# An implicit-filter convolution with a scored normalization: two orders changed in a software-pipelined loop over channels

## The chip, the cores and the metric

The kernel runs on one core of a Trainium2 chip. The metric is the device time of one launch in microseconds (us), as a median over runs. "Slot" below means four 64x64 matmuls that use the four quarters of the TensorE array at the same time.

## What is computed

For each of C = 64 channels, four images of 256 x 256 (float32) go through two layers. Layer 0 makes, from two small sine networks, one filter per axis, hx and hy; their outer product is a 2D filter, applied as a causal 2D convolution, and a bias times the input is added. Layer 1 forms scores of the rows, weighs and sums them, adds the sums to the rows, and normalizes each channel over all images.

```python
k = einsum('ijk,imk->ijmk', hx, hy)[0]                  # hx, hy: decayed sine networks
y = irfft2(rfft2(x, 512) * rfft2(k, 512) / 512)[:256, :256]   # causal 2D convolution
x = y + x * bias[:, None, None]
scores = einsum('bpsd,bptd->bpst', x, x) / sqrt(256)
red = sum(scores * weights[None], axis=-1, keepdims=True)
y = x + red
mean, var = mean(y, (0, 2, 3)), var(y, (0, 2, 3))       # per channel
out = (y - mean) * rsqrt(var + 1e-5) * gamma + beta
```

The filter being separable, the 2D convolution is two 1D convolutions, each a matrix product with a Toeplitz matrix.

## The kernel before

**Data.** A channel's four images lie as [128 partitions, 2 pairs v, 4 column groups, 256], two images in the two halves of the partitions. The filters are computed once, written to DRAM (g_dram), and each channel's Toeplitz tile (toep, `hs[c]`, four buffers) is read from there by four DMAs of 52 KB (`load_h`, L203) into partitions 0 to 63; `copy_h` (L208) copies them to partitions 64 to 127 on ScalarE (ACT). The input comes in four DMAs of 256 KB per channel (`load_xt`, L76), the weights in one of 320 KB (`load_w`, L82, on ACT's DMA queue), and the result leaves in four DMAs of 256 KB (`finish`, L616 and its DMA L617).

**The order is written by hand.** The scheduler is off; every engine runs its instructions in the order in which the program lists them. A loop over c = 0 to 61 works, in each pass ("period"), on several channels at once: the first convolution z of channel c+1, the second convolution x0 of channel c, G (the scores) of channel c, and the sums, the normalization and the output of channels c-1 to c-4 (in the code p, q, f, e).

**TensorE (PE) in one period**, 52 slots:
1. x0, first half (`conv_x0`, `x0_slots`, L323): 8 slots of 256, 192, 128, 64, 256, 192, 128, 64 columns into the PSUM tile p2_0.
2. x0's second half (p2_1) alternating with z's first half (`z_slots`, L263, p1_0, 8 slots of 256, 128, 64, 64 columns twice over): 16 slots.
3. z's second half (p1_1): 8 slots.
4. G's first half (`gram`, L392): four slots of 192 columns, four of 128.
5. G's second half: the same 8 slots, with four slots of 64 columns of the *shared product* for channel c+2 among them (`shared_slots`, L234). `take` draws from both in turn until the shorter is used up.

The shared product is a part of z that two block rows have in common: the sum of two column groups (`sums`, L225, on VectorE) times one Toeplitz block. `keep_shared` (L243) copies it from PSUM to SBUF on ACT, and `add_shared` (L278, VectorE) adds it to z in the next period.

**PSUM** is one pool of four slots of two banks each, shared by p2_0, p2_1, p1_0, p1_1, the two G tiles and the shared product. Each slot is handed on when its last reader is done.

**VectorE (DVE) in one period:** `add_bias` (L344) of x0's two halves, `add_red` (L499) twice, L278 twice, small steps of the normalization, and `weigh_pair` on each G tile (four L429 and one L418), with `turn_rows` (a transpose, L463) in the second.

**ACT:** an output at five places in the period, `parts_of(c, 0)` to `parts_of(c, 4)` (place 4 is empty but for the last channels), `pick_red` (L492), `root` (three small steps), `copy_h`, the copies of z (L272), the mean and the squares (L547 to L552), and, at the end, `keep_shared`.

**GpSimd (POOL):** `sum_squares` (L558), the accumulating DMA `add_rows` (L473), `sum_means` (L505) and the long reduction `all_sum` (L483), which `pick_red` of the next period reads.

**The rows' way.** `keep_rows` writes the transposed row sums to DRAM from SyncE's (SP's) queue (L468); `add_rows` on POOL adds them into pr from there; `all_sum` then reduces pr. SP issues, in this order: rows, first output, xt, two Toeplitz loads, output, xt, two Toeplitz loads, output, xt, output, xt. An output's DMA waits there for ACT, the rows' for DVE, with all later ones behind it.

Of the kernel before, what the change touches and what calls it, by code (L numbers as in the profile page):

```python
# [15 lines left out]
B, C, S = 4, 64, 256  # L16
# [25 lines left out]
def conv_scores_bn_kernel(  # L42
# [29 lines left out]
    def load_xt(c, v, n):  # L72
        if c not in xts:
            xts[c] = ld.tile([P, 2, 4, S], F32, tag="xt", name=f"xt_{c}", bufs=4)
        part = bass.ts(n, 2)
        nc.sync.dma_start(xts[c][:, v, part], xT[c, v, :, part])  # L76
# [117 lines left out]
    def load_h(c, n):  # L194


        if not n:
            hs[c] = ld.tile([P, ROW], F32, tag="toep", name=f"toep_{c}", bufs=4)
        src = bass.AP(
            g_dram.tensor, g_dram.offset + c * GL + 16 * n,  # L200
            [[4 + C * GL, COPIES], [1, 4], [1, ROW]],
        )
        nc.sync.dma_start(hs[c][bass.ts(n, 16)], src)  # L203
# [12 lines left out]
    def pair_of_banks(name):  # L216
        return ps.tile([P, 2, 2, S], F32, tag="ps", name=name)
# [9 lines left out]
    def shared_slots(c, both):  # L227

        toep = hs[c].rearrange("p (b s) -> p b s", s=H)
        for k in range(4):  # L230
            for t in range(4):
                u, v = t % 2, t // 2
                rows = bass.ts(u, H)
                nc.tensor.matmul(  # L234
                    both[bass.ts(v, H), u, k], lhsT=xss[c][rows, v, bass.ts(k, H)],
                    rhs=toep[rows, 11], start=(k == 0), stop=(k == 3),
                )
            yield

    def keep_shared(c, both):  # L240

        kept[c] = wk.tile([P, 2, 2, P], F32, tag="kept", name=f"kept_{c}")
        nc.scalar.copy(  # L243
            kept[c].rearrange("p m u s -> p u m s"),
            both[:, :, :4].rearrange("p u (m k) s -> p u m (k s)", k=2),
        )
# [57 lines left out]
    def take(*slots):  # L304

        slots = list(slots)
        while slots:
            slots = [s for s in slots if next(s, s) is None]

    def copy_z_plain(c, m, p1):  # L310
        for u in range(2):
            nc.scalar.copy(zs[c][:, m, u], p1[:, u, :, ::-1])

    def x0_slots(c, z, m, p2):


        toep = hs[c]
        for i in range(2):
            for k in range(4):
                for t in range(4):  # L320
                    v, u = t % 2, t // 2
                    rows = bass.ts(v, H)
                    nc.tensor.matmul(  # L323
                        p2[bass.ts(u, H), v, i, : S - H * k],
                        lhsT=z[rows, k // 2, u, k % 2, bass.ts(2 * m + i, H)],
                        rhs=toep[rows, H * k : S], start=(k == 0), stop=(k == 3),
                    )
                yield

    def conv_x0(c, z, m):  # L330
        p2 = pair_of_banks(f"p2_{c}_{m}")
        take(x0_slots(c, z, m, p2))
        return p2
# [35 lines left out]
    def begin(c):  # L369
        x0 = wk.tile([P, 2, 4, S], F32, tag="x0", name=f"x0_{c}", bufs=5)  # L370
        red0 = reds[c % 3][:, : 2 * B].rearrange("p (b n) -> p b n", n=2)
        sp = wk.tile([P, B, S], F32, tag="sp", name=f"sp_{c}")
        pr = wk.tile([P, B, S], F32, tag="pr", name=f"pr_{c}")
        rd = wk.tile([P, B, S], F32, tag="rd", name=f"rd_{c}")
        st8[c] = (x0, red0, sp, pr, rd)
# [3 lines left out]
    def gram_slots(c, v, gs):  # L379


        xb = st8[c][0].rearrange("p v i (t s) -> p v i t s", s=H)
        for places in (
            ((0, slice(0, 3), slice(0, 5, 2)), (1, slice(1, 4), slice(2, 7, 2))),
            ((2, slice(2, 4), slice(3, 7, 3)), (3, slice(0, 4, 3), slice(0, 4, 3))),
        ):
            for i in range(4):
                for n in range(4):
                    u, h = n % 2, n // 2
                    rows = bass.ts(u, H)  # L390
                    m, t, o = places[h]
                    nc.tensor.matmul(  # L392
                        gs[bass.ts(h, H), u, o, :],
                        lhsT=xb[rows, v, i, m, :], rhs=xb[rows, v, i, t, :],
                        start=(i == 0), stop=(i == 3),
                    )
                yield
# [67 lines left out]
    def keep_rows(c):  # L465

        rows[c] = dram.tile([P, 32], F32, name=f"rows_{c}")
        nc.sync.dma_start(rows[c], acrosses.pop(c))  # L468

    def add_rows(c):  # L470

        pr = st8[c][3]
        nc.gpsimd.dma_start(  # L473
            pr[0:1].rearrange("p b (n q i) -> p (b n) q i", n=2, i=32),
            rows.pop(c).rearrange("(q j) i -> j q i", q=4)[None, : 2 * B], accum_op=ALU.add,
        )
# [11 lines left out]
    def pick_red(c, v=None):  # L488

        rd = st8[c][4].rearrange("p (v u) s -> p v u s", u=2)  # L490
        pairs = slice(0, 2) if v is None else v
        nc.scalar.copy(rd[H:, pairs, 0, :], rd[H:, pairs, 1, :])  # L492
# [63 lines left out]
    def sum_squares(c, mom):  # L556
        tot = sm.tile([P, 3], F32, tag="tot", name=f"tot_{c}")
        nc.gpsimd.partition_all_reduce(tot[:, 0:2], mom[:, 6:8], P, RED.add)  # L558
        return tot
# [248 lines left out]
    def begin_z(c):  # L808
        zs[c] = wk.tile([P, 2, 2, 2, S], F32, tag="z", name=f"z_{c}")
# [21 lines left out]
    for c in range(C - 2):  # L831
        p, q, f = c - 1, c - 2, c - 3
        short = c + 1 > 1
        begin(c)
        begin_z(c + 1)
        z = zs.pop(c)
        if p >= 0:
            keep_rows(p)
        if f >= 0:
            tot = sum_squares(f, moms[f])  # L840
        if p >= 0:
            add_rows(p)
        parts_of(c, 0)
        if c + 3 < C:
            load_xt(c + 3, 0, 0)
            for n in range(2):
                load_h(c + 3, n)
        if c:
            p2 = conv_x0(c, z, 0)
            add_bias(c, 0, p2)  # L850
        else:
            first_x0(z)
        if q >= 0:
            pick_red(q)
        if f >= 0:
            scales[f] = root(f, tot)
            steps = scale_steps(f, moms.pop(f), *scales.pop(f))
        else:
            steps = iter(())
        parts_of(c, 1)  # L860
        if c + 3 < C:
            load_xt(c + 3, 1, 0)
            for n in range(2, 4):
                load_h(c + 3, n)
        copy_h(c + 2)
        if c + 2 < C - 1:
            sums(c + 2)
        if q >= 0:
            add_red(q, 0)
        next(steps, None)  # L870
        slots = []
        if c:
            p2 = pair_of_banks(f"p2_{c}_1")
            slots.append(x0_slots(c, z, 1, p2))
        p1 = [pair_of_banks(f"p1_{c + 1}_0")]
        slots.append((z_slots if short else plain_slots)(c + 1, 0, p1[0]))
        take(*slots)
        copy_any = copy_z if short else copy_z_plain
        copy_any(c + 1, 0, p1[0])
        if c:  # L880
            add_bias(c, 1, p2)
        next(steps, None)
        parts_of(c, 2)
        if c + 3 < C:
            load_xt(c + 3, 0, 1)
        if q >= 0:
            add_red(q, 1)
            sum_means(moms[q])
        if p >= 0:
            all_sum(p)  # L890
        next(steps, None)
        p1.append(pair_of_banks(f"p1_{c + 1}_1"))
        take((z_slots if short else plain_slots)(c + 1, 1, p1[1]))
        copy_any(c + 1, 1, p1[1])
        load_w(c + 1, nc.scalar)
        for m in range(2):
            if short:
                add_shared(c + 1, m, p1[m])
            next(steps, None)
        for _ in steps:  # L900
            pass
        if q >= 0:
            minus_mean(moms[q])
            squares(q, moms[q], 0)
        parts_of(c, 3)
        if c + 3 < C:
            load_xt(c + 3, 1, 1)
        if q >= 0:
            squares(q, moms[q], 1)
        parts_of(c, 4)  # L910
        gram(c, 0)
        slots = []
        if c + 2 < C - 1:
            both = ps.tile([P, 2, 8, H], F32, tag="ps", name=f"shared_{c + 2}")
            slots.append(shared_slots(c + 2, both))
        gs = gram_banks(c, 1)
        take(gram_slots(c, 1, gs), *slots)
        if c + 2 < C - 1:
            keep_shared(c + 2, both)
        weigh_pair(c, 1, gs)  # L920
    last_channels(C - 1)

# [70 lines left out]
```

## Time and profile before

| what | value |
|---|---|
| median of 3 runs | 911.4 us (910.69 to 915.17) |
| the profiled execution | 910.59 us, span 908.7 us |
| mean granted TensorE clock | 0.992 |
| PE busy, weight loads (PEld) busy | 95%, 89% |
| DVE, ACT, POOL busy | 79%, 68%, 53% |
| DMA | 175.56 MB, mean 193 GB/s |

The span runs from the first to the last instruction of the profiled execution; its own time is 1.9 us longer. In the timelines a line gives start and duration in us, engine, line of the kernel, operation, what is written and read, shapes and a count, and in brackets how long the engine stood idle before it and what released it. In the waits a line gives who waited for what, the total in us, the number of waits and the longest. "issue" is time in which an engine waited for nothing that the profile shows. The fp32 matmuls appear as two weight loads and two matmuls each.

### The profile page before, as it was taken

The page shows a single profiled execution, that of the slowest core. Times are in us where ns is not written, and L with a number is a line of the kernel's source. Part 1 is how long each engine was busy: PE and PEld are TensorE (multiplying, and loading weights), DVE is VectorE, ACT ScalarE, POOL GpSimd, SP SyncE. Part 2 cuts the span into 40 slices and gives each one's busy share as a digit, 9 for nine tenths or more (in the row PEclk, how much of TensorE's full clock was granted, in tenths as well). Part 3 has the DMA queues.
Part 4 walks back from the last instruction along what each step waited for, and adds up shares of the span by engine and source line. Part 5 has one row for each costly group of instructions (what it writes and reads, how often), then busy time and mean ns, then how long its engine had stood idle before and what let it go on. Part 6 is the DMA issues. An engine that isn't in the chain of part 4 may idle for free.

```text
span 908.7 us, 59198 instructions
## 1 busy us (share of the span) xinstructions
PE 866.6 (95%) x26626; PEld 809.6 (89%) x26626; DVE 720.1 (79%) x2160; ACT 616.9 (68%) x1157; POOL 479.7 (53%) x255
## 2 busy tenths in 40 slices
PE   7999999999999999999999999999999999989995
PEld 5899999999998989999989989998888889889994
DVE  3478888878878878878888888887787878878787
ACT  2247677767767766767767767767767767676687
POOL 0065566556556546556546646546546546465540
PEclk9999999999999999999999999999999999999997
DMA  6545666656665655656666666665655655656535
GB/s 191 170 126 184 201 208 203 210 187 203 213 188 192 223 186 187 217 181 216 214 195 196 217 192 193 206 203 189 203 189 188 218 188 185 193 180 205 169 134 187
DMA packets 103545, 175.56 MB, mean 193 GB/s; under 512 B 24219, under 2 KB 25148, under 8 KB 103292
## 3 DMA queue, kind: packets, MB, share of 16 engines
q1 hardware_dynamic: 88828, 150.33, 50.4%
q10 hardware_dynamic: 9584, 21.17, 7.7%
q8 instruction: 209, 3.42, 1.6%
q0 software_dynamic: 4880, 0.27, 0.7%
q14 instruction: 44, 0.36, 0.1%
HBM read 102.56 MB, written 69.03 MB: 189 GB/s over the span
## 4 chain that ended last, share of the span: by engine, by line
PE 91%; issue 3%; DVE 3%; DMA 1%; ACT 1%; SPq 0%; DVEq 0%; ACTq 0%
PE g L392 31%; PE p L323 30%; PE p L263 25%; PE shared L234 3%; DMA g_dram<-g_sb 1%; PE p L292 1%; DVE x L339 1%; DMA fw_sb<-in_fw 0%; DVE junk L429 0%; DMA toep<-g_dram 0%; DVE x L541 0%; DVE x L499 0%; SPq L203 0%; PE ph L157 0%; PE ph L141 0%
## 5 line engine op out<-in xcount | busy, mean ns | idle before, releaser
L323 PE MATMUL p<-toep,z 64*64 64x256 f32 (+3 forms) x8064 | 386.8, 297 | 2.9 <-issue 2.7
L483 POOL PARTITION_ALL_REDUCE rd<-pr x61 | 377.8, 6193 | 3.1 <-DMA pr<-rows 3.1
L392 PE MATMUL g<-x 64*64 64x192 f32 (+1 forms) x8192 | 339.2, 297 | 13.0 <-issue 11.7
L263 PE MATMUL p<-toep,xt 64*64 64x64 f32 (+2 forms) x7808 | 336.3, 271 | 6.5 <-issue 6.3
L323 PEld LDWEIGHTS p<-toep,z 64*64 64x64 f32 x8064 | 313.3, 133 | 20.5 <-issue 10.0
L392 PEld LDWEIGHTS g<-x 64*64 64x64 f32 x8192 | 285.3, 133 | 25.7 <-issue 21.4
L263 PEld LDWEIGHTS p<-toep,xt 64*64 64x64 f32 x7808 | 286.0, 133 | 22.2 <-issue 11.9
L429 DVE SCALAR_TENSOR_TENSOR junk<-g,w 128x192 f32<-128x192 f32 x512 | 152.4, 353 | 91.1 <-PE g L392 90.1
L344 DVE SCALAR_TENSOR_TENSOR x<-xt,chan_sb,p 128x1024 f32<-128x1024 f32 x122 | 156.2, 1280 | 66.8 <-PE p L323 66.6
L616 ACT ACTIVATE o<-x,sh,g 128x512 f32<-128x512 f32 x252 | 202.5, 807 | 0.3 <-DVE sh L604 0.3
L272 ACT COPY z<-p 128x512 f32<-128x512 f32 x122 | 71.5, 586 | 137.5 <-PE p L263 137.5
L505 POOL PARTITION_ALL_REDUCE mom<-mom x62 | 24.2, 391 | 256.8 <-DVE x L499 253.9
L499 DVE SCALAR_TENSOR_TENSOR x<-x,rd 128x1024 f32<-128x1024 f32 x122 | 148.4, 1217 | 0.0
L552 ACT ACTIVATE sq<-x,mom 128x1024 f32<-128x1024 f32 x127 | 145.0, 1142 | 2.1
L473 POOL DMA_DIRECT2D pr<-rows x61 | 54.2, 888 | 142.7 <-DMA rows<-across 65.8
L234 PE MATMUL shared<-toep,xs 64*64 64x64 f32 x1952 | 102.0, 218 | 2.0 <-issue 1.8
L234 PEld LDWEIGHTS shared<-toep,xs 64*64 64x64 f32 x1952 | 98.5, 133 | 6.0 <-issue 4.5
L492 ACT COPY rd<-rd 64x512 f32<-64x512 f32 (+1 forms) x62 | 37.9, 612 | 74.1 <-POOL rd L483 74.0
L418 DVE SCALAR_TENSOR_TENSOR pr<-g,w 128x512 f32<-128x512 f32 x126 | 84.1, 668 | 0.0
L278 DVE TENSOR_TENSOR z<-p,kept 128x512 f32<-128x512 f32 x122 | 83.0, 681 | 0.7 <-ACT z L272 0.6
L208 ACT COPY toep<-toep 64x832 f32<-64x832 f32 x63 | 55.7, 885 | 10.5 <-DMA toep<-g_dram 9.0
L225 DVE TENSOR_TENSOR xs<-xt 128x512 f32<-128x512 f32 x61 | 41.8, 685 | 4.5 <-DMA xt<-in_xT 4.2
(100 smaller groups left out, 434.7 us busy)
## 6 DMA issues: line engine op xcount, KB each, us to landing
xt<-in_xT SPq DMA_DIRECT2D x256, 256.0 KB
out<-o SPq DMA_DIRECT2D x256, 256.0 KB
w<-in_wl ACTq DMA_DIRECT2D x62, 320.0 KB
toep<-g_dram SPq DMA_DIRECT2D x252, 52.0 KB
rows<-across SPq DMA_DIRECT2D x61, 16.0 KB
pr<-rows POOLq DMA_DIRECT2D x61, 4.0 KB, 3.6
w<-in_wl SPq DMA_DIRECT2D x2, 320.0 KB
g_dram<-g_sb ACTq DMA_DIRECT2D x1, 576.0 KB
```

Source lines behind the costliest of these rows:

```text
L234: nc.tensor.matmul(both[bass.ts(v, H), u, k], lhsT=xss[c][rows, v, bass.ts(k, H)], rhs=toep[rows, 11], start=(k == 0), stop=(k == 3),)
L263: nc.tensor.matmul(out[:, outs], lhsT=xts[c][rows, v, i, bass.ts(2 * m + k, H)], rhs=toep[rows, cols], start=(i == 0), stop=(i == 3),)
L278: nc.vector.tensor_tensor(z[:, :, :1:-1, ::-1], y[:, :, :2], part[:, :, None, :].to_broadcast([P, 4, 2, H]), ALU.add,)
L323: nc.tensor.matmul(p2[bass.ts(u, H), v, i, : S - H * k], lhsT=z[rows, k // 2, u, k % 2, bass.ts(2 * m + i, H)], rhs=toep[rows, H * k : S], ...
L344: nc.vector.scalar_tensor_tensor(st8[c][0][:, :, part], xts[c][:, :, part], chan_sb[:, 0, c : c + 1], p2[:, :, :, ::-1], ALU.mult, ALU.add,)
L392: nc.tensor.matmul(gs[bass.ts(h, H), u, o, :], lhsT=xb[rows, v, i, m, :], rhs=xb[rows, v, i, t, :], start=(i == 0), stop=(i == 3),)
L418: nc.vector.scalar_tensor_tensor(pr[:, 2 * v : 2 * v + 2].rearrange("p u (t s) -> p u t s", s=H), both[:, :, COL, :], 1.0 / math.sqrt(S), ...
L429: nc.vector.scalar_tensor_tensor(junk, g[:, part, :], 1.0 / math.sqrt(S), w[:, 3 * n : 3 * n + 3, :], ALU.mult, ALU.mult, accum_out=red0[: ...
L483: nc.gpsimd.partition_all_reduce(rd[:, part].rearrange("p b s -> p (b s)"), sp[:, part].rearrange("p b s -> p (b s)"), P, RED.add,)
L499: nc.vector.scalar_tensor_tensor(x0[:, v], x0[:, v], 1.0, rd[:, 2 * v, None, :].to_broadcast([P, 4, S]), ALU.mult, ALU.add, accum_out=moms ...
L552: nc.scalar.activation(sq, st8[c][0][:, v], AF.Square, bias=mom[:, 5:6], accum_out=mom[:, 6 + v : 7 + v])
L616: nc.scalar.activation(o, y, AF.Identity, bias=sh, scale=g)
```

## The change

Three edits, all in the loop. (1) `keep_rows` and `add_rows` move behind `parts_of(c, 0)` and the first xt load. On SP's queue the first output and the first xt load so come before the rows; on POOL `add_rows` still follows `sum_squares`. (2) The four Toeplitz loads of a channel, two behind the first and two behind the second xt load until now, are issued together behind the last xt load of the period, which itself follows the output of place 3. (3) The four shared slots no longer alternate with the first slots of G's second half. The new `take_with` draws one shared slot after every fourth slot of its main sequence: two in G's second half (after the 4th and the 8th) and two in the next period's x0, first half (after the 4th and the 8th). `keep_shared` moves with them, behind that x0 half, so that on ACT it now stands between the first output and `pick_red`. Slots, matmuls, DMAs and copies are the same in number and size.

```diff
+    def take_with(slots, between):
+
+        for n, _ in enumerate(slots):
+            if n % 4 == 3:
+                next(between, None)
...
         z = zs.pop(c)
-        if p >= 0:
-            keep_rows(p)
         if f >= 0:
             tot = sum_squares(f, moms[f])
-        if p >= 0:
-            add_rows(p)
         parts_of(c, 0)
         if c + 3 < C:
             load_xt(c + 3, 0, 0)
-            for n in range(2):
-                load_h(c + 3, n)
+        if p >= 0:
+            keep_rows(p)
+            add_rows(p)
         if c:
-            p2 = conv_x0(c, z, 0)
+            p2 = pair_of_banks(f"p2_{c}_0")
+            take_with(x0_slots(c, z, 0, p2), shared)
+            if short:
+                keep_shared(c + 1, both)
             add_bias(c, 0, p2)
...
         parts_of(c, 1)
         if c + 3 < C:
             load_xt(c + 3, 1, 0)
-            for n in range(2, 4):
-                load_h(c + 3, n)
         copy_h(c + 2)
...
         parts_of(c, 3)
         if c + 3 < C:
             load_xt(c + 3, 1, 1)
+            for n in range(4):
+                load_h(c + 3, n)
...
         gram(c, 0)
-        slots = []
+        shared = iter(())
         if c + 2 < C - 1:
             both = ps.tile([P, 2, 8, H], F32, tag="ps", name=f"shared_{c + 2}")
-            slots.append(shared_slots(c + 2, both))
+            shared = shared_slots(c + 2, both)
         gs = gram_banks(c, 1)
-        take(gram_slots(c, 1, gs), *slots)
-        if c + 2 < C - 1:
-            keep_shared(c + 2, both)
+        take_with(gram_slots(c, 1, gs), shared)
         weigh_pair(c, 1, gs)
```

## The prediction

> **What bounds the kernel now.** I read the page first: engine busy times, the DMA queues, the chain that ended last.
>
> ```profile
> PE 866.6 (95%) x26626; PEld 809.6 (89%) x26626; DVE 720.1 (79%) x2160; ACT 616.9 (68%) x1157; POOL 479.7 (53%) x255
> ...
> q8 instruction: 209, 3.42, 1.6%
> ...
> PE 91%; issue 3%; DVE 3%; DMA 1%; ACT 1%; SPq 0%; DVEq 0%; ACTq 0%
> ```
>
> PE carries the end. What it waits for is "issue", in which nothing shown releases it. The waits view between 90 and 850 us puts numbers to it:
>
> ```profile
> PEld g L392 <- issue: 20.7, 33, 1.8
> PEld p L263 <- issue: 11.9, 24, 1.1
> PE g L392 <- issue: 11.7, 22, 1.5
> PEld p L323 <- issue: 8.9, 20, 1.1
> ```
>
> With the shared product's 4.3 the weight loads stood 45.8 us for issue in these 57 periods, and for no data longer than 0.4 us. The q8 row says what issue is. PE ran 2 x 26626 = 53252 instructions over 209 fetches, 255 each: code comes in blocks of 256. Numbering PE's instructions by start, every weight-load stop above 0.5 us from 90 us until the tail falls on a number with remainder 193 or 194 by 256. Two neighbours in PE's timeline, one block apart:
>
> ```profile
> 461.71 0.48 PE L263 MATMUL p<-toep,xt 64*64 64x128 f32 x15 [0.46 <-issue]
> ...
> 466.10 0.27 PE L234 MATMUL shared<-toep,xs 64*64 64x64 f32 x2 [0.35 <-issue]
> ```
>
> So PE enters a block, the next one's fetch starts (median 1.42 us later by the DMA packets, ended at 2.63), and it can be run 1.2 to 1.6 us after that. I call the whole the latency L: quartiles 3.77, 4.04 and 4.31 us over 182 blocks. Where a block runs out before L, PE stops.
>
> The other engines are read from one undisturbed period (414.73 to 427.45, 12.72 us), in the timelines of ACT, POOL, DVE and SP:
>
> ```profile
> 414.95 0.56 ACT L243 COPY kept<-shared 128x512 f32<-128x512 f32 x1
> 415.42 0.81 ACT L616 ACTIVATE o<-x,sh,g 128x512 f32<-128x512 f32 x1
> 417.50 0.61 ACT L492 COPY rd<-rd 64x512 f32<-64x512 f32 x1 [1.27 <-POOL rd L483]
> ...
> 418.84 0.89 POOL L473 DMA_DIRECT2D pr<-rows  x1 [0.98 <-DVE x L344]
> 423.69 0.39 POOL L505 PARTITION_ALL_REDUCE mom<-mom  x1 [3.97 <-DVE x L499]
> 423.99 6.20 POOL L483 PARTITION_ALL_REDUCE rd<-pr  x1
> ...
> 416.34 0.65 DVE L418 SCALAR_TENSOR_TENSOR pr<-g,w 128x512 f32<-128x512 f32 x1
> 417.15 1.28 DVE L344 SCALAR_TENSOR_TENSOR x<-xt,chan_sb,p 128x1024 f32<-128x1024 f32 x1 [0.16 <-PE p L323]
> ...
> 416.44 0.32 SPq L468 DMA_DIRECT2D rows<-across  x1
> ```
>
> ACT, POOL and DVE each show idle time in a period in which PE shows none.
>
> **The shared slots, costed as code blocks.** The change removes and adds no matmul. A slot is 16 PE instructions, so a block is 16 slots; a period has 52 slots and 7424 columns. At 12.71 us (the undisturbed period) a column takes 1.712 ns, and a block C = columns x 1.712 ns. Over four periods the 13 blocks before hold 1984 to 2624 columns, 3.40 to 4.49 us: the narrow shared slots stand together in the first half of G's second product, so blocks there run out early. Spread, they hold 2048 to 2432, 3.51 to 4.16 us. The mean excess of L over C, taken over the 182 values, is 0.65 us at C = 3.4, 0.47 at 3.6, 0.32 at 3.8, 0.19 at 4.0, 0.10 at 4.2, 0.04 at 4.5. Summed over the blocks and averaged over the four places at which blocks can begin, a period loses 0.901 us before and 0.863 after. Measured: the 61 kept copies (L243) start from 37.2 to 854.4 us, 13.62 each, so 0.91 above 12.71. The model holds. Gain: 0.038 x 61 = 2.3 us. By the single starting places it is 5.7, 0.4, -0.5 and 3.7; multi-wait instructions shift the place from period to period, so I take the mean.
>
> The Trainium skill's "Runtime: NRT & Kernel Launch", Instruction fetch mechanics, says that the next page is fetched while the current one executes and that crossing a block boundary is mostly hidden. By that rule alone this edit would be worth nothing; the 45.8 us of issue above contradict it here.
>
> **The product's banks and its copy.** The four-slot pool hands out the slot released longest ago. keep_shared (L243) now follows the weighing of G's second half, so p1_0 inherits G's slot and p1_1 the shared one. p1_0's first matmul stands behind the rest of G (1 shared slot), 8 x0 slots, 2 shared and one more x0 slot: 0.11 + 2.19 + 0.22 + 0.44 = 2.96 us at 1.712 ns. DVE frees G's slot 2.0 us after it starts (414.97 to 416.99), which lies about 0.25 behind the last G matmul. 0.7 us of cover, so zero. The copy, 0.56 us, leaves ACT's tail; at the head it waits for x0's last slot, where L344 starts (417.15), and holds pick_red (L492), root, an output and copy_h behind it. pick_red moves from 417.50 to about 417.7 here, and by 1.2 in the period before (x0 over at 404.44, pick_red at 403.71). add_red (L499), its reader, starts 1.74 us after it in the median. Zero. Without that cover each us would be one on DVE before the second add_bias.
>
> **SP's queue.** The first output, already first on ACT, no longer waits for the rows. But rows (L468) now stand behind xt, four Toeplitz loads, the output and another xt. From the xt issue's end at 415.57: 4 x 0.63 + 0.47 + 0.50 = 419.1, against 416.44, so 2.6 us later, and up to 3.6 with the transfers queued ahead. Queued behind them: add_rows (L473), its DMA (3.6 us to landing), all_sum (L483), pick_red, add_red, add_bias, G. Cover: all_sum starts about 1.9 us after its data, pick_red to add_red 1.74, DVE idle 0.73 before the second add_bias, G 0.35 behind that (medians of 50 periods): 4.7 us. Cost zero, between 0 and 0.5 us in a tail of periods; POOL's new wait will show. The last Toeplitz load is issued by 418.1 and lands some 2 to 3 us later (its packets ended 2.1 us after the issues of 417.83), about 420 to 421; copy_h (L208) wanted it at 419.69, and the copy behind it has 0.5 idle before it and 2 us until its reader is late. Zero again; bounds 0 and 0.3 us a period.
>
> The row for the Toeplitz loads' own speed: the two issued from 417.83 had their packets from about 419.3 to 421.2, 1.9 us for 104 KB. The skill's "DMA: Bandwidth & Descriptors" (Why a DMA increments its semaphore by 16 and not by 1) has a DMA use the largest number of engines up to 16 that divides the slowest dimensions on both sides, the lowest-numbered first; the source here begins with 4 copies, so four loads in a row would queue 52 KB on each of the same four engines. By the page's 436 GB/s over 16 engines rows would come up to 1.9 us later still (an estimate), 4.5 to 5.5 us against the cover of 4.7: the rule speaks against this move, no view of this trace separates engines, and the sum above does without it.
>
> **Sum.** 910.59 (profiled execution; span 908.7, 1.9 around it) - 2.3 = 908.3. The median of the three runs is 0.8 above that execution: 909 on their scale.
>
> **Rivals.** What the trace can't price is L after the DMA issues move: a period's 13 SP issues are the same bytes in another order. A shift of L acts on 3.25 fetches x 61 periods x 0.59 (share of L above C) = 117 us per us.
> - Slower: outputs and xt loads now gather with the weights' load at the period's end and run into the Toeplitz group, and fetches wait in busier stretches. In the trace L averages 4.22 with the DMA engines 75 to 90% busy and 3.93 below 60%. At +0.1 us, +12 - 2 = 920; it turns the sign from +0.02.
> - Faster: the quiet stretch at the period's head (46 to 56 KB/us against 193 mean) is filled and the middle thinned; L -0.08 gives -9 - 2 = 899.
> - p1_0 gets the shared slot after all: PE then stands for end of the last shared slot, 0.2 latency, 0.56 copy, less the one x0 slot (0.44): 0.32 x 61 = 20 us, 20 - 2 above 910.6: 928.
> - The spread does nothing, stops merely move: 911.
>
> **Numbers.** My forecast (with the do-nothing case) 0.45, slower by L or a late chain 0.27, faster by L 0.23, the bank wait 0.05. The forecast alone would hold 905 to 913; with the others 898 to 922. Half a per cent, 4.6 us, is what a measurement of this kernel can tell: faster by more 0.33, within 0.38, slower 0.29.
>
> **What would show it.** Right: undisturbed periods stay at 12.7 us; PEld's issue total falls by 2 us; ACT waits for L243 and briefly for the Toeplitz DMA; POOL's all_sum waits for pr. Wrong: a PE wait at L263 for ACT or DVE, L492 late enough to hold L344, or fetch packets ending above 2.65 us (or below 2.55) after block entry.

## The result and the profile after

The change is slower. Its median is 924.32 us (922.56 to 926.51, four runs) against 912.31 us for the kernel before on the same chip: a ratio of 1.0129 (1.0091 to 1.0168). The forecast was 909 us on the scale of the medians, in a range of 898 to 922; the time lies just above the range, and the sign was wrong. Ratios here and below leave out single executions that were more than 1.5% above the fastest of the same kernel on the same chip; the medians include them.

The page of the changed kernel (span 920.7 us, its execution 922.56 us): busy time of each engine, the queue that fetches PE's code, the chain that ended last by engine and by line, the costliest group, the landing time of the accumulating DMA. Lines of the loop are six higher than before (L344 is now L350, L392 is L398, L468 is L474, L473 is L479, L483 is L489, L492 is L498, L499 is L505).

```profile
PE 863.6 (94%) x26626; PEld 788.1 (86%) x26626; DVE 741.5 (81%) x2160; ACT 616.4 (67%) x1157; POOL 482.3 (52%) x255
...
q8 instruction: 209, 3.42, 1.6%
...
PE 42%; DMA 18%; POOL 17%; DVE 11%; issue 5%; ACT 4%; SPq 2%; ACTq 0%; POOLq 0%; DVEq 0%
...
L489 POOL PARTITION_ALL_REDUCE rd<-pr x61 | 373.8, 6128 | 140.9 <-DMA pr<-rows 140.9
...
pr<-rows POOLq DMA_DIRECT2D x61, 4.0 KB, 4.5
```

The page of before has for the last two:

```profile
L483 POOL PARTITION_ALL_REDUCE rd<-pr x61 | 377.8, 6193 | 3.1 <-DMA pr<-rows 3.1
...
pr<-rows POOLq DMA_DIRECT2D x61, 4.0 KB, 3.6
```

PE executes the same number of instructions and fetches the same 209 blocks of code, but it carries 42% of the chain that ended last, where it carried 91%. DMA, POOL and DVE have taken the rest: all_sum (L489) now waits 140.9 us for its data, where it waited 3.1 us. The waits between 90 and 850 us (who waited for what, total us, times, longest):

```profile
ACT rd L498 <- POOL rd L489: 138.1, 55, 6.0
POOL rd L489 <- DMA pr<-rows: 131.8, 51, 4.9
DVE x L505 <- ACT rd L498: 71.1, 48, 1.7
...
PEld g L398 <- DVE x L350: 25.9, 22, 2.4
PE g L398 <- DVE x L350: 18.4, 20, 2.0
...
PEld p L329 <- issue: 11.8, 19, 1.6
PEld p L263 <- issue: 8.1, 21, 1.2
PEld g L398 <- issue: 7.7, 14, 1.2
```

From top to bottom this is a chain: the rows' sums arrive late, so all_sum, pick_red and add_red start late, so the second add_bias (L350) does, and G waits for it. Before, PE's waits for data in this window came to 0.4 us. Its stops for code ("issue") became fewer. Here and below PE's stops are the idle times above 0.1 us ahead of its weight loads, over the whole span: 50.6 us for code before; 35.0 us for code and 27.7 us for data after. Their sum grew by 12.1 us, the span by 12.0.

The turn of that chain with the longest of these stops, from SP's, POOL's, ACT's, DVE's and PEld's timelines of the changed kernel (start us, duration us; in brackets the idle time before, and what ended it):

```profile
214.98 0.21 DVE L469 STREAM_TRANSPOSE across<-reds 128x32 f32<-128x32 f32 x1
...
215.58 2.58 SPq L203 DMA_DIRECT2D toep<-g_dram  x4
218.26 0.38 SPq L623 DMA_DIRECT2D out<-o  x1
218.74 0.68 SPq L76 DMA_DIRECT2D xt<-in_xT  x1
219.52 0.42 SPq L474 DMA_DIRECT2D rows<-across  x1
...
223.32 0.89 POOL L479 DMA_DIRECT2D pr<-rows  x1 [3.79 <-DMA rows<-across]
223.94 0.65 POOL L511 PARTITION_ALL_REDUCE mom<-mom  x1
229.45 6.12 POOL L489 PARTITION_ALL_REDUCE rd<-pr  x1 [4.86 <-DMA pr<-rows]
...
235.61 0.61 ACT L498 COPY rd<-rd 64x512 f32<-64x512 f32 x1 [6.02 <-POOL rd L489]
...
236.25 1.23 DVE L505 SCALAR_TENSOR_TENSOR x<-x,rd 128x1024 f32<-128x1024 f32 x1 [1.72 <-ACT rd L498]
...
237.48 1.26 DVE L350 SCALAR_TENSOR_TENSOR x<-xt,chan_sb,p 128x1024 f32<-128x1024 f32 x1
...
238.79 1.29 PEld L398 LDWEIGHTS g<-x 64*64 64x64 f32 x40 [2.39 <-DVE x L350]
```

The transpose is done at 215.2; SP is then busy with four Toeplitz loads, an output and an xt load until 219.4. The rows leave at 219.52, add_rows goes 3.8 us later, and all_sum starts 6.1 us after add_rows. Each step from there starts within 0.05 us of the end of the one before it, and G stands for 2.39 us. In the period that the prediction shows of before, all_sum starts 7.6 us after the rows' issue; here it is 9.9, with the issue 4.3 us behind the transpose in addition.

### The profile page after: what moved, and what is told of

It is laid out like the page before. It is cut to its first block, busy times and chain, and to the rows that moved or that the text cites. A ratio compares the mean times of both kernels' runs of the same rounds, so it can differ in the third digit from the quotient of the medians.

```text
span 920.7 us, 59140 instructions
## 1 busy us (share of the span) xinstructions
PE 863.6 (94%) x26626; PEld 788.1 (86%) x26626; DVE 741.5 (81%) x2160; ACT 616.4 (67%) x1157; POOL 482.3 (52%) x255
## 4 chain that ended last, share of the span: by engine, by line
PE 42%; DMA 18%; POOL 17%; DVE 11%; issue 5%; ACT 4%; SPq 2%; ACTq 0%; POOLq 0%; DVEq 0%
POOL rd L489 17%; PE g L398 15%; PE p L329 14%; DMA pr<-rows 13%; PE p L263 10%; DVE x L505 4%; DMA rows<-across 3%; DVE x L350 2%; ACT rd L498 2%; PE shared L234 2%; SPq L203 1%; ACT o L622 1%; DMA toep<-g_dram 1%; DVE junk L435 1%; DMA g_dram<-g_sb 1%
## 5 line engine op out<-in xcount | busy, mean ns | idle before, releaser
L489 POOL PARTITION_ALL_REDUCE rd<-pr x61 | 373.8, 6128 | 140.9 <-DMA pr<-rows 140.9
L329 PE MATMUL p<-toep,z 64*64 64x256 f32 (+3 forms) x8064 | 393.7, 298 | 7.3 <-issue 6.9
L398 PE MATMUL g<-x 64*64 64x192 f32 (+1 forms) x8192 | 313.9, 297 | 25.0 <-DVE x L350 19.5
L263 PE MATMUL p<-toep,xt 64*64 64x64 f32 (+2 forms) x7808 | 326.2, 271 | 3.8 <-issue 3.3
L329 PEld LDWEIGHTS p<-toep,z 64*64 64x64 f32 x8064 | 302.6, 134 | 31.1 <-issue 13.6
L398 PEld LDWEIGHTS g<-x 64*64 64x64 f32 x8192 | 270.9, 133 | 44.7 <-DVE x L350 27.4
L263 PEld LDWEIGHTS p<-toep,xt 64*64 64x64 f32 x7808 | 269.4, 133 | 25.9 <-issue 9.0
L505 DVE SCALAR_TENSOR_TENSOR x<-x,rd 128x1024 f32<-128x1024 f32 x122 | 148.7, 1220 | 75.7 <-ACT rd L498 75.6
L350 DVE SCALAR_TENSOR_TENSOR x<-xt,chan_sb,p 128x1024 f32<-128x1024 f32 x122 | 155.4, 1273 | 33.6 <-PE p L329 33.3
L435 DVE SCALAR_TENSOR_TENSOR junk<-g,w 128x192 f32<-128x192 f32 x512 | 151.6, 351 | 21.9 <-PE g L398 21.7
L479 POOL DMA_DIRECT2D pr<-rows x61 | 54.2, 889 | 208.5 <-DMA rows<-across 63.2
L498 ACT COPY rd<-rd 64x512 f32<-64x512 f32 (+1 forms) x62 | 37.9, 612 | 146.5 <-POOL rd L489 146.4
L234 PE MATMUL shared<-toep,xs 64*64 64x64 f32 x1952 | 92.0, 219 | 2.8 <-issue 2.8
L243 ACT COPY kept<-shared 128x512 f32<-128x512 f32 x61 | 35.8, 586 | 74.0 <-PE shared L234 74.0
L234 PEld LDWEIGHTS shared<-toep,xs 64*64 64x64 f32 x1952 | 78.2, 134 | 5.2 <-issue 3.6
L225 DVE TENSOR_TENSOR xs<-xt 128x512 f32<-128x512 f32 x61 | 67.1, 1100 | 18.5 <-DMA xt<-in_xT 13.0
L272 ACT COPY z<-p 128x512 f32<-128x512 f32 x122 | 70.9, 581 | 10.8 <-PE p L263 9.3
L208 ACT COPY toep<-toep 64x832 f32<-64x832 f32 x63 | 55.7, 884 | 22.4 <-DMA toep<-g_dram 20.2
```

The lines of the kernel that those rows point to most:

```text
L234: nc.tensor.matmul(both[bass.ts(v, H), u, k], lhsT=xss[c][rows, v, bass.ts(k, H)], rhs=toep[rows, 11], start=(k == 0), stop=(k == 3),)
L263: nc.tensor.matmul(out[:, outs], lhsT=xts[c][rows, v, i, bass.ts(2 * m + k, H)], rhs=toep[rows, cols], start=(i == 0), stop=(i == 3),)
L329: nc.tensor.matmul(p2[bass.ts(u, H), v, i, : S - H * k], lhsT=z[rows, k // 2, u, k % 2, bass.ts(2 * m + i, H)], rhs=toep[rows, H * k : S], ...
L350: nc.vector.scalar_tensor_tensor(st8[c][0][:, :, part], xts[c][:, :, part], chan_sb[:, 0, c : c + 1], p2[:, :, :, ::-1], ALU.mult, ALU.add,)
L398: nc.tensor.matmul(gs[bass.ts(h, H), u, o, :], lhsT=xb[rows, v, i, m, :], rhs=xb[rows, v, i, t, :], start=(i == 0), stop=(i == 3),)
L435: nc.vector.scalar_tensor_tensor(junk, g[:, part, :], 1.0 / math.sqrt(S), w[:, 3 * n : 3 * n + 3, :], ALU.mult, ALU.mult, accum_out=red0[: ...
```

## The experiments

The question was which of the three edits costs time, and by which way: theory A, the late rows; or PE's code fetches, made longer by the order of the other DMAs, which the other theories in the expectations hold in several forms. Each group (e1 to e4, e5 to e8, e9 to e12, e13 and e14, e15 to e17) ran on one chip with the kernel before beside it; its medians there were 907.28, 912.76, 915.15, 900.21 and 915.57 us, so times are compared as ratios within a group. Stops are those of one profiled execution, and the kernel before was profiled on two chips only: 50.6 us for code on the first, 59.4 on that of e15. For the other groups its stops can be estimated as its median there, less 1.9, less 858 us (span less stops, below): 47 us for e1 to e4, 53 for e5 to e8, 55 for e9 to e12, 40 for e13 and e14. Stops for code are to be held against these. "For data" are PE's waits on the rows' chain; others come to 2 us at most, in e10 to 6. "Way" is the median time from the transpose's end to the start of all_sum, between 90 and 850 us.

| kernel | what it has | ratio to before (95%) | stops for code | for data | way |
|---|---|---|---|---|---|
| before | – | 1 | 50.6 | 0 | 7.6 |
| e3 | edit 3 | 0.992 (0.9883–0.9958) | 42.0 | 0 | 8.2 |
| e14 | edits 1, 3, rows on ACT's queue | 1.010 (1.0045–1.0156) | 46.6 | 0 | 8.4 |
| e1 | edit 1 | 1.0062 (1.0031–1.0093) | 56.1 | 0 | 8.5 |
| e2 | edit 2 | 1.0078 (1.0042–1.0115) | 56.1 | 0 | 8.5 |
| e5 | edits 2, 3 | 1.0005 (0.9969–1.0041) | 52.1 | 0 | 8.9 |
| e6 | edits 1, 3 | 1.0121 (1.0087–1.0155) | 63.3 | 0 | 9.0 |
| e13 | all, rows on ACT's queue | 1.0065 (1.0028–1.0102) | 40.8 | 0 | 9.0 |
| e4 | edits 1, 2 | 1.0129 (1.0091–1.0166) | 41.3 | 14.2 | 10.8 |
| e16 | all, again | 1.0101 (1.0055–1.0148) | 46.3 | 20.7 | 11.7 |
| after | all | 1.0129 (1.0091–1.0168) | 35.0 | 27.7 | 12.0 |
| e9 | all, rows on POOL's queue | 1.0309 (1.0275–1.0343) | 45.2 | 32.7 | 12.2 |
| e10 | edit 3, rows far later | 1.1844 (1.1812–1.1875) | 7.9 | 157.5 | 17.5 |

Read down, the last two columns show a threshold: up to 9.0 us the way costs PE nothing, from 10.8 on it does.

**e1: edit 1 alone** (against the kernel before).

```diff
-        if p >= 0:
-            keep_rows(p)
...
-        if p >= 0:
-            add_rows(p)
         parts_of(c, 0)
...
             load_xt(c + 3, 0, 0)
+        if p >= 0:
+            keep_rows(p)
+            add_rows(p)
```

> The kernel before with the first edit alone: rows behind the first output and the first xt load, the Toeplitz loads two and two at their old places. Theory A (the rows' chain: rows, pr, all_sum, pick_red, add_red, add_bias, G comes too late when rows stand behind four Toeplitz loads and an output and an xt load): rows issue about 0.9 us later than before, well inside the cover of 4.7 us, so the time stays within 0.4% of before (909 to 915), POOL waits for pr under 25 us in all and G for add_bias under 3. Theory B (keep_shared at ACT's head holds pick_red): no such copy here, within 0.4% of before. Theory C (code fetches get slower by the new order of the data DMAs): a small part at most, 0 to +4 us with fetch stops above 50 us.

0.6% slower, where at most 0.4% was expected, with no wait for data: the rows' move does not break the chain by itself. More stops for code come out instead (56.1 us, against about 47 by the estimate); between 60 and 860 us, 15 fetches had their last packet more than 3.6 us after the block was entered, against 4 in the profile of before. The mean end of the packets did not move (2.65 us after entry in both).

**e2: edit 2 alone.**

```diff
             load_xt(c + 3, 0, 0)
-            for n in range(2):
-                load_h(c + 3, n)
...
             load_xt(c + 3, 1, 0)
-            for n in range(2, 4):
-                load_h(c + 3, n)
...
             load_xt(c + 3, 1, 1)
+            for n in range(4):
+                load_h(c + 3, n)
```

> The kernel before with the second edit alone: all four Toeplitz loads behind the last xt load, rows again first in the period. Theory A: rows wait only for the end of the four Toeplitz issues, 1.5 to 2 us behind the transpose, plus about 1 us in the queues: 3 to 4 us of the 4.7 are used; within 0.5% of before, POOL's waits for pr 20 to 80 us, G's waits for add_bias 0 to 6 us. Theory B: within 0.4% of before. Theory C: the whole of the loss, +8 to +12 us, with fetch stops above 55 us.

0.8% slower, in the same manner: no wait for data, 56.1 us for code, 15 long fetches.

**e3: edit 3 alone** (against the kernel before); the DMAs keep their order.

```diff
-            p2 = conv_x0(c, z, 0)
+            p2 = pair_of_banks(f"p2_{c}_0")
+            take_with(x0_slots(c, z, 0, p2), shared)
+            if short:
+                keep_shared(c + 1, both)
...
-        take(gram_slots(c, 1, gs), *slots)
-        if c + 2 < C - 1:
-            keep_shared(c + 2, both)
+        take_with(gram_slots(c, 1, gs), shared)
```

> The kernel before with the third edit alone: shared slots spread, keep_shared at ACT's head; rows and Toeplitz loads at their old places. Theory A: no loss; 2 us faster by fewer fetch stops (905 to 912). Theory B: most of the loss of the whole change, +8 to +12 us, with pick_red held by L243 and add_bias waiting for add_red. Theory C: no loss, -2 to 0.

0.8% faster. The stops for code total 42.0 us, the lowest of the three single edits. This is the one edit that gains by itself.

**e4: edits 1 and 2**, the diffs of e1 and e2 together.

> The first two edits together without the third: rows behind four Toeplitz loads, an output and an xt load; the shared slots as before. Theory A: the whole loss or a little more, +10 to +16 us, POOL's waits for pr above 110 us, G's waits for add_bias 15 to 35 us. Theory B: within 0.4% of before. Theory C: +8 to +12 us, but with fetch stops above 55 us and few waits for add_bias.

1.3% slower, as much as the whole change. From the waits of e4 between 90 and 850 us:

```profile
ACT rd L498 <- POOL rd L489: 184.7, 56, 5.5
POOL rd L489 <- DMA pr<-rows: 113.0, 53, 4.2
...
DVE x L505 <- ACT rd L498: 45.3, 37, 1.7
...
PEld g L398 <- DVE x L350: 8.4, 10, 1.7
```

The chain is late, as in the whole change, and without the spread. It takes the two moves together: each alone leaves the way at 8.5 us, both make it 10.8.

**e5: the whole change with the rows first again** (edits 2 and 3), and **e6: with the Toeplitz loads back in their two pairs** (edits 1 and 3).

```diff
         z = zs.pop(c)
+        if p >= 0:
+            keep_rows(p)
...
+        if p >= 0:
+            add_rows(p)
         parts_of(c, 0)
         if c + 3 < C:
             load_xt(c + 3, 0, 0)
-        if p >= 0:
-            keep_rows(p)
-            add_rows(p)
```

> The whole change with its first edit undone: rows first in the period again, the Toeplitz loads still behind the last xt load, the shared slots spread. Theory A (G waits for add_bias because the rows come late): the data waits of the whole change (27.7 us of G for add_bias) fall below 5 us; about +8 - 7 = +1 us against before (within 0.5%), 10 us faster than the whole change. Rival B' (the waits come from keep_shared at ACT's head, which the spread brings in): they stay above 15 us and the time stays at +1.0% or more.

```diff
             keep_rows(p)
             add_rows(p)
+        if c + 3 < C:
+            for n in range(2):
+                load_h(c + 3, n)
...
             load_xt(c + 3, 1, 0)
+            for n in range(2, 4):
+                load_h(c + 3, n)
...
             load_xt(c + 3, 1, 1)
-            for n in range(4):
-                load_h(c + 3, n)
```

> The whole change with its second edit undone: rows behind the first output and xt load, Toeplitz loads at their old places, shared slots spread. Theory A: data waits below 5 us; +6 - 7 = -1 us against before (within 0.5%). Rival B': data waits above 15 us, +1.0% or more.

Both take the wait for data away. e5 comes back to the time of before, as the late rows would have it. e6 does not: it is 1.2% slower with no wait for data, and its stops for code are the most of all, 63.3 us against an estimated 53. So edit 1 costs something that is not the rows' lateness, and the theory of late rows, taken alone, missed here.

**e7: the kernel before with the weights' load later**, between `minus_mean` and the squares, and **e8: the same with edit 3**. Many of the long fetches begin just after an output, an xt and the weights' load have been issued within about 1.5 us (11 of e2's 15); e7 and e8 pull that bunch apart.

```diff
-        load_w(c + 1, nc.scalar)
...
             minus_mean(moms[q])
+        load_w(c + 1, nc.scalar)
+        if q >= 0:
             squares(q, moms[q], 0)
```

> The kernel before with one thing moved: the weights' load (320 KB) issued about 2 us later in the period, between the mean and the squares on ACT, into the gap behind the third output and xt load instead of beside them. Theory D (PE's long code fetches, with packets ending over 3.6 us after block entry, are those that fall into the bunch of weights, output and xt load): fetch stops fall by 4 to 10 us, the fetches entered in the bunch go from 2.8 us to 2.6, time -0.4 to -1.1%. Rival (fetch latency depends on the bytes in the period alone): no change, within 0.3%.

> The third edit alone and the weights' load moved as in e7. Theory D: both gains, -1.2 to -1.9% against before (890 to 897 on the scale on which before has 907). Rival: as the third edit alone, -0.8%.

e7 is slower, 1.0059 (1.0024 to 1.0093). e8 stands at 0.9994 (0.9968 to 1.002), where edit 3 alone gained 0.8% on another chip. Neither is faster than without the move, as they should have been if that bunch held the fetches.

**e9: the whole change, rows' DMA on POOL's queue**, and **e10: edit 3 with the rows behind the second output and xt load**.

```diff
-        nc.sync.dma_start(rows[c], acrosses.pop(c))
+        nc.gpsimd.dma_start(rows[c], acrosses.pop(c))
```

```diff
-        if p >= 0:
-            keep_rows(p)
...
-        if p >= 0:
-            add_rows(p)
         parts_of(c, 0)
...
             load_xt(c + 3, 1, 0)
+        if p >= 0:
+            keep_rows(p)
+            add_rows(p)
```

> The whole change with one word changed: the rows' DMA is issued from POOL's own queue instead of SP's, so it no longer stands behind the Toeplitz loads, the output and the xt load in SP's order; every other instruction keeps its place. Theory A (whole change: late rows): G's waits for add_bias fall from 27.7 us to below 5. What the time does then tells whether the whole change's few fetch stops (35 us) are its own or only covered by the data waits: if its own, 12 to 20 us faster than the whole change (about -0.3 to -0.9% against before); if only covered, they return to 45 to 60 us and the time stays at 0 to +1% against before. Rival (late rows are not the cause): data waits stay above 15 us, +1.3%.

> The third edit alone, and the rows moved behind the second output and xt load (Toeplitz loads at their old places), so that they come late by another way: about 4 us behind the transpose. Theory A: POOL's all_sum waits for pr above 100 us, data waits on PE 25 to 60 us, +1.5 to +4% against before. Rival (fetch latency alone decides, whatever the rows do): data waits below 5 us, fetch stops 50 to 65 us, 0 to +1.2%.

e9 was meant to free the rows from SP's queue and made them later. POOL's timeline shows why:

```profile
413.19 6.12 POOL L489 PARTITION_ALL_REDUCE rd<-pr  x1 [2.59 <-DMA pr<-rows]
419.23 0.48 POOL L564 PARTITION_ALL_REDUCE tot<-mom  x1
419.58 0.59 POOL L474 DMA_DIRECT2D rows<-across  x1
422.77 0.87 POOL L479 DMA_DIRECT2D pr<-rows  x1 [2.60 <-DVE u L582]
```

On POOL the rows stand behind `sum_squares` (L564), and that behind the late all_sum of the period before: once late, the chain keeps itself late, and the rows leave 4.2 us behind the transpose in the median. The run can't say what a free queue is worth; e13 does. e10 delays the rows on purpose: they left 9.9 us behind the transpose, where 4 were meant. The time grew by 18%, far more than expected: 157.5 us of PE's waits for add_bias, and span less stops of 916 us, at a granted clock of 0.935 in this execution (0.992 before). PE stood for code hardly at all (7.9 us). While PE waits for data, its code arrives.

**e11: keep_shared alone moved** behind x0's first half, slots alternating as before, and **e12: no weights' loads in the loop**; channels 1 to 62 use the weights of the first.

```diff
             p2 = conv_x0(c, z, 0)
+            if short:
+                keep_shared(c + 1, both)
             add_bias(c, 0, p2)
...
         take(gram_slots(c, 1, gs), *slots)
-        if c + 2 < C - 1:
-            keep_shared(c + 2, both)
         weigh_pair(c, 1, gs)
```

```diff
-        load_w(c + 1, nc.scalar)
+        ws[c + 1] = ws[c]
```

> The kernel before with only keep_shared moved from ACT's tail to behind x0's first half (the four shared slots stay together in G). It splits the gain of the third edit (-0.8% alone, of which evener code blocks should make only 0.25%). If the evener blocks make the gain: no change here, within 0.3% of before, fetch stops 48 to 56 us. If the new order on ACT (outputs issued earlier or later, so another latency of the fetches) makes it: -0.4 to -0.8%, mean packet end after block entry below 2.62 us.

> The kernel before without the weights' loads of the loop (320 KB a period left out, channels 1 to 62 use the first channel's weights); PE's work and every wait but that load's stay. Theory C (PE's stops are code fetches held up by the data DMAs): mean packet end after block entry falls by 0.1 to 0.3 us, fetch stops from 50 to 20 to 40 us, -1 to -3.3%. Rival (stops come from the fetch itself, whatever else the DMA engines carry): within 0.4% of before.

e11 changes nothing: 0.9989 (0.9954 to 1.0024). Its 60.1 us for code lie above the 48 to 56 expected, with only 5 fetches ending later than 3.6 us, so such late fetches are not what the stops mainly consist of. The copy's move gains nothing alone; the gain of edit 3 needs its slots. e12 removes 320 KB a period, no PE instruction, and is 1.6% faster, 0.9837 (0.9795 to 0.988). Its waits between 90 and 850 us:

```profile
PEld g L392 <- issue: 17.4, 35, 1.3
PEld p L263 <- issue: 9.6, 19, 1.0
PEld p L323 <- issue: 5.2, 12, 1.0
...
PEld shared L234 <- issue: 3.8, 10, 0.8
```

Over the whole span the stops for code are 38.1 us, against 60.1 in e11 on the same chip, and the packets between 90 and 850 us ended 2.60 us after entry in the mean, against 2.70. With less data moved, PE stands less for code: data in flight hold up the fetches.

**e13: the whole change, rows' DMA on ACT's queue**, and **e14: the same without edit 2**.

```diff
         rows[c] = dram.tile([P, 32], F32, name=f"rows_{c}")
-        nc.sync.dma_start(rows[c], acrosses.pop(c))
+        nc.scalar.dma_start(rows[c], acrosses.pop(c))
```

> The whole change with the rows' DMA issued from ACT's queue, behind the first output and ahead of keep_shared, where ACT waits for x0 anyway: rows leave right behind the transpose and depend on no other issue (from POOL's queue, e9, they waited for all_sum itself). All other instructions as in the whole change. Theory A (data waits by late rows): rows 0.1 to 0.4 us behind the transpose instead of 3.2; G's waits for add_bias below 5 us. If the whole change's few fetch stops (35 us) are its own: fetch stops 30 to 42, -1 to -1.8% against before. If data waits had only covered them: fetch stops 48 to 65, -0.2 to +1.2%. Rival (keep_shared at ACT's head or the banks make the data waits): they stay above 15 us.

> e6 (rows behind the first output and xt load, shared slots spread, Toeplitz loads at their old places; +1.2% with no data waits, 63 us of fetch stops) with the rows' DMA on ACT's queue. If e6 loses because the first output and xt load leave earlier, no longer held by the rows, and meet the code fetches: unchanged, fetch stops 55 to 70, +0.8 to +1.5%. If it loses because the rows and the pr DMA behind them leave later: back to the spread alone, fetch stops 38 to 48, -0.3 to -1.1%.

In e13 the rows leave 0.7 us behind the transpose instead of 3.2, everything else as in the whole change. Its waits between 90 and 850 us:

```profile
POOL rd L489 <- DMA pr<-rows: 35.0, 27, 2.5
...
DVE x L505 <- ACT rd L498: 10.1, 15, 1.6
```

No wait of PE for add_bias is left; DVE's wait for pick_red has gone from 71.1 to 10.1 us. The rows' place in SP's queue is therefore the cause of PE's waits for data. The time is still 1.0065 (1.0028 to 1.0102): about half of the loss stays (the whole change lost 1.3 and 1.0% on its two chips), with no wait for data. As span less stops keeps its value (857.4 us), this half can only be stops for code; the trace doesn't show them, since its execution (900.15 us) was faster than e13's median (903.41) and has 40.8 us for code, no more than the estimate for before. e14 suggests that this half isn't due to the rows or the Toeplitz loads: with the one out of SP's queue and the others in their old places, the first output and xt load ahead of where they were still go with 1.0% more time (1.0045 to 1.0156), edit 3's gain included. No run has the rows on ACT's queue and all else as before, so that this issue itself costs something isn't excluded. Both kernels fell between the cases set out for them: the times are those of the one case, the stops (40.8, 46.6 us) in the band of the other. The bands came from other chips; on this one before has some 40 us.

**e15, e16, e17: the kernel before, the whole change and edit 3 alone, on one chip**, so that stops for code can be compared.

> The kernel before, profiled on the same chip as the next two: span = 858 us plus PE's stops (for code, no data waits), as in its first profile.

> The whole change beside the kernel before and the spread alone, on one chip. If the late rows cost what they show: data waits 15 to 35 us, fetch stops 5 to 20 us fewer than e15's, 858 plus both as the span, +1.0 to +1.6% against before. If the loss were fetch latency alone: data waits below 5 us and fetch stops 8 to 15 us above e15's.

> The third edit alone on the same chip: no data waits, fetch stops 4 to 10 us below e15's, -0.4 to -1.1% against before. If its gain in e3 was the chip's, within 0.3%.

e15, a single run, has 59.4 us for code and a span of 919.0; e16 46.3 for code and 20.7 for data, span 925.4; e17 52.3 for code, span 909.0. From before to the whole change that is 13.1 less for code and 20.7 more for data, +7.6 where the span grew by 6.4. From before to edit 3 it is 7.1 less, where the span fell by 10.0. Both ratios repeat: 1.0101 for the whole, 0.9952 (0.9919 to 0.9985) for edit 3, the version that beats both kernels.

## Why the prediction was wrong

**What bounds the kernel: right for the kernel before.** Span less stops is 858.1 us before and 858.0 after, and 856 to 862 in the variants (e10, at a lower clock, is left out). e12 confirms the bound with PE's work unchanged. The Trainium skill, "Runtime: NRT & Kernel Launch", Instruction fetch mechanics, calls a block crossing mostly hidden; 50.6 us of a span of 908.7 speak against it for this stream of matmuls.

**The shared slots: right in sign, probably too small.** 2.3 us were predicted; the ratios give 7.3 us (3.8 to 10.6, e3) and 4.4 (1.4 to 7.4, e17), nearer to the best of the single starting places (5.7 to −0.5) than to their mean, which I took; e17's interval still holds the 2.3. Since the copy alone gains nothing (e11), the gain needs the slots' new places. That it is the evenness of the blocks that does it is the model's reading; no run varied the evenness by itself.

**Banks, copy, Toeplitz loads: right.** PE doesn't wait at L263 for ACT or DVE, and in e3, where the copy sits at ACT's head, PE doesn't wait for data. copy_h (L208) waits longer for its loads, 20.2 us in all against 9.0; that none of it reached PE is read from e2 and e5, where all four loads are last and PE doesn't wait for the rows' chain or the loads.

**SP's queue: the step that failed.** It read "2.6 us later, and up to 3.6 with the transfers queued ahead" against a cover of 4.7, and "Cost zero, between 0 and 0.5 us in a tail of periods". The cover fits. Before, the way is 7.6 us, 1.9 of it slack ahead of all_sum, so 5.7 + 4.7 = 10.4 us is where it should begin to cost, and the table puts the point between 9.0 and 10.8. The delay was mis-sized. Medians, before to after: the rows leave 0.03, then 3.19 us behind the transpose (2.6 said). From their issue to add_rows it is 2.13, then 3.96: 1.8 more, where at most 1.0 was allowed. The accumulating DMA lands after 3.6, then 4.5 us, and I had left that at 3.6. Together 3.2 + 1.8 + 0.9 = 5.9 against 4.7. I counted issue times and one line of transfers ahead of the rows; but two small DMAs stand one behind the other, and both took longer. For the first, the traffic moved in front of it fits: in the 2 us after the rows' issue the DMA engines were 85% busy in the median, 40% before. It isn't the whole of it, since e2 and e13 have 49 and 45% there and still 3.6 and 3.9 us to add_rows; and in the 3 us after add_rows the share is nearly the same (78 and 73%), so what lengthens the second isn't shown. e1 shows the first apart: there the rows leave only 0.5 us later, and add_rows follows them 2.2 us later than before (4.35 against 2.13). I had this number within reach: the estimate by the skill's "DMA: Bandwidth & Descriptors" (Why a DMA increments its semaphore by 16 and not by 1), 4.5 to 5.5 us, reached over the cover, and I let it stand aside. Its total is nearer the measurement than mine; no run here separates the engines, so that its mechanism acts isn't shown.

The excess of the median way over 10.4 us is 1.6 us, 98 us in 61 periods, and PE lost 27.7 us. G waited in 22 of some 57 periods only. In the program's order the chain from a channel's transpose to G of the channel after next runs through two periods, so a stop of PE in one also gives time to the chain under way for the next; how much of the difference this makes isn't settled.

**The rivals.** The sum also held L at its old value, since the trace couldn't price it; "slower by L" stood beside it as a rival, and by e13 it was about half of the truth: e1, e2, e6, e7 and e14 lose 0.6 to 1.2% without any wait for data, so the order of DMAs alone moves PE's stops for code by as much as edit 3 gains. In the whole change this doesn't show: PE's waits for data give the code time to arrive (35.0 us for code against 50.6), and the fetch packets ended earlier after entry, not later (2.56 us in the mean against 2.65; 2.61 in e16 against 2.71 in e15). So the named sign, packets ending above 2.65 us, did not come. I had put "a late chain" under the same 0.27 but priced it at nothing of its own; L492 late enough to hold L344 was named as a sign of being wrong, and it is what came. In the changed kernel's trace the waits for data are the whole of the 12 us; e13 shows that with them gone only about half of the time comes back.

**What stays open.** Which property of the DMAs' order lengthens fetches. e7 and e8 speak against the bunch with the weights; e6 and e14 point to the output and xt load that come earlier, but no run shows how these two reach a fetch. Nor is it settled why e1 (+0.6%) and e3 (−0.8%) together make +1.2% (e6).

## What to carry to other kernels

Before a small DMA is moved behind large ones in an issuing queue, sum its whole way to the consumer (issue, landing, the next DMA's landing) with each landing lengthened by the traffic put ahead, and hold that against the slack; where two estimates of the delay lie on both sides of the slack, the cost isn't zero. Here the small DMA did best at the head of SP's queue; on ACT's it no longer made PE wait for data, and on POOL's, which holds part of the chain that it feeds, it came later still. Where the busiest engine stops for code, a reordering of DMAs that changes no byte can move the time by 1%, and pieces of a change must be timed apart: here one gained 0.5 to 0.8% by itself, while each of the others lost 0.6 to 0.8%.

## What the runs showed of the hardware

`sums` (L225, a VectorE add of two SBUF tiles, 0.685 us) took 1.10 us in the mean and up to 3.35 in the changed kernel. From its POOL and DVE timelines:

```profile
229.45 6.12 POOL L489 PARTITION_ALL_REDUCE rd<-pr  x1 [4.86 <-DMA pr<-rows]
...
231.18 3.35 DVE L225 TENSOR_TENSOR xs<-xt 128x512 f32<-128x512 f32 x1 [1.02 <-DMA toep<-g_dram]
```

The late all_sum now lies over it. In 27 periods the add began between 1.7 and 4.3 us after all_sum's start and was stretched, and in every one of them it ended 5.08 us after that start; begun 4.4 us or more after it, it took its usual 0.69. DVE's scalar_tensor_tensor instructions under all_sum kept their times (L435 0.352 us with and without). The skill's "SBUF — State Buffer" (Terms) has GpSimd and VectorE share a port pair that one holds for the full instruction while the other is blocked; this trace agrees that the add is held up, but it is free again at 5.08 us, before the recorded 6.12 us are over (recorded spans on POOL are rough). It cost nothing here: add_red follows 1.72 us later, released by pick_red.

The kernel before differed by 1.7% between chips (900.21 to 915.57 us), more than any single edit was worth.
